# A four-layer cross-attention kernel: output projections joined two by two in PSUM, grouped layers one step later, the grouped maximum spread in SBUF

## The chip, the cores and the metric

The kernel runs on one core of one Trainium2 chip. The metric is the device time of one execution in microseconds; a run is one timed execution, and the time of the kernel before is the median of three.

## The reference, cut to what matters

Four layers of cross-attention follow each other on four sequences (b = 0 to 3) of 512 positions with 256 channels. The keys and values of all layers come from one context of 1024 positions with 512 channels for each sequence. Layers 0, 2 and 3 have 16 heads of 64 and add a penalty to four chosen keys; they are called masked below. Layer 1 has 16 query heads of 16, which share 4 key and value heads, and a root-mean-square norm ahead of the query projection; it is called grouped.

```python
# masked layer (0, 2, 3)
q = x @ Wq;  k = ctx @ Wk;  v = ctx @ Wv          # split in 16 heads of 64
logits = q k^T / 8 + col_bias                       # -20 * (1 - mask) on chosen keys
x = softmax(logits) @ v @ Wo + bo + x
# grouped layer (1)
xn = x * rsqrt(mean(x * x) + eps) * norm_w
q = xn @ wq;  k = ctx @ wk;  v = ctx @ wv           # 16 query heads, 4 shared key heads
x = x + softmax(q k^T / 4) @ v @ wo
```

All is computed in float32.

## The kernel before, in words

**Groups and steps.** A layer of a sequence is cut into eight groups (`units`): a masked group is a pair of heads, a grouped group is half of the query heads of one place r in all shared heads (h = 0 or 1). `order` puts them into 96 steps by two strings written by hand: MASKED_TURNS names the sequence whose next masked group is scored in a step, GROUPED_TURNS the sequence of its grouped group, if there is one. 96 steps have a masked group, 32 of them a grouped one too. Layers of one sequence follow each other, since a layer's query projection needs the full result of the layer before.

**What a step does.** In the loop over n, `g` is the masked group of the step, `g1` that of the step before, `lam` the grouped group, `coming` the grouped group of the next step, `follows` the masked group of the next step, `soon` the grouped group two steps on.

- `scores(g)` (L622): eight tiles of 128 keys by two heads of 512 queries. L632 multiplies into a pair of PSUM banks, ACT copies the tile to SBUF (L642), and DVE folds it into a running maximum which stays in the banks of the first tile (L646).
- DVE reduces that maximum over keys (L683, L691, L716) and `max_everywhere` spreads it over two banks (L723); eight subtractions (L728) and eight exponentials (L734) follow, and POOL adds up the exponentials (L773).
- TensorE meanwhile multiplies g1's exponentials by the values (`attend`, L662). In a step with `lam`, its scores (L611) and exponentials (L619) go pair by pair between those of g1.
- `reciprocal_sums` and `scale_out` (L787 to L815) normalise g1's product into a tile `ot`; `normalise_grouped` (L775) does so for a grouped pair that was finished in the step before (`turned`).
- `project_out` (L817) multiplies `ot` by the output weights (four matmul instructions L829) into two banks, and DVE adds them to the layer's accumulator (L851). Both happen in the step after the group was normalised. A grouped output is projected after every second grouped group.
- `project_q` (L533, matmul L543) makes the queries of the next masked group and of coming grouped ones; `k_part` (L467, grouped L485) and the value functions (L509) make keys and values.
- `maxima_pair` (L597) computes the scores of the coming grouped group once for its maximum alone; `lower_queries` (L694) reduces it, spreads it with a transposition into one PSUM bank (L706) and lowers the queries by it (L709). The bank is then given back.

**Order of the work.** The schedule is manual: each engine takes its instructions in the order in which the program issues them. `scores`, the attention of g1 and the exponentials of lam are issued first. Then a list `fill` of TensorE work is issued item by item; each has a planned length in microseconds, and DVE and ACT work is issued when the planned clock passes its due time (`events`: subtraction t at 0.7 + 1.2 t, exponential t at 3.3 + 1.22 t; `pairs`: grouped maxima from 11.0 or 12.0 on). The add behind a projection is issued when its item is done.

**PSUM.** `Place` hands out one or two of the eight banks. It takes the free bank (or pair) that was given back longest ago; `late` makes a returned bank count as returned later. So which bank a tile gets, and on whose last read it waits, follows from the order of the returns.

**Loads.** `load_masked` issues on SP, at the start of a step, the key weights of the group three steps on, the query weights two on, g's output weights (L442, four buffers) and the value weights two on.

Of the kernel before, what the change touches and what calls it, by code (L numbers as in the profile page):

```python
# [42 lines left out]
def units(b):  # L43
# [13 lines left out]
    "000000001111111122222222000000001111111100000000"  # L57
    "222222223333333311111111222233333333222233333333"
)
GROUPED_TURNS = (  # L60
    "...........00000000..11111111..22222222........."
    "...................33333333....................."
)
# [13 lines left out]
def kernel(ctx: ExitStack, tc: tile.TileContext, a: dict, out: bass.AP):  # L77
# [616 lines left out]
    def lower_queries(g):  # L694


        half = max_halves(g, g.mx)
        every = t_([P, S // 32, 1], "every1", f"every1_{g.name}")
        for c in range(4):
            cols = slice(c % 2 * S // 32, (c % 2 + 1) * S // 32)  # L700
            nc.vector.tensor_tensor(
                every[32 * c : 32 * (c + 1), :, 0], half[0:32, cols], half[32:64, cols], ALU.max
            )
        w = Place(1)
        m = w.ap
        nc.vector.transpose(  # L706
            m.rearrange("p (b r) -> p b r", r=32), every.to_broadcast([P, S // 32, 32])
        )
        nc.vector.scalar_tensor_tensor(g.qt, m, row16[:, 1:2], g.qt, ALU.mult, ALU.add)  # L709
        w.back(late=2)  # L710

# [63 lines left out]
    def normalise_grouped(g, m):  # L775
# [7 lines left out]
        )  # L783
        g.ot = t_([P, S], "ot", f"ot_{g.name}", bufs=3)
        nc.vector.tensor_tensor(g.ot, o, m, ALU.mult)

# [29 lines left out]

    def project_out(g):  # L817
        x, acc = xs[g.l, g.b], xs.get((g.l + 1, g.b))
# [9 lines left out]
        for k in range(KC):  # L828
            nc.tensor.matmul(  # L829
                m[:, k * S : (k + 1) * S], lhsT=g.wo[:, k * P : (k + 1) * P], rhs=g.ot,  # L830
                start=True, stop=True,
            )
        y = m.rearrange("p (k q) -> p k q", q=S)
# [19 lines left out]

        left[g.b] -= 1
        return add
# [36 lines left out]
    def masked_at(n):  # L892
        return masked[n] if n < len(masked) else None

    def head(g):
# [52 lines left out]
    count = 0  # L948
    ready = []
    turned = []  # L950
    left = {b: 32 - 4 for b in range(B)}

    for n in range(len(steps) + 2):
# [8 lines left out]
        def load_masked():  # L962
            if g and masked_at(g.n + 3):
                load_k(masked_at(g.n + 3))
            if g and masked_at(g.n + 2):
                load_q(masked_at(g.n + 2))
            if g:
                load_o(g)
            if g and masked_at(g.n + 2):
                load_v(masked_at(g.n + 2))  # L970
# [14 lines left out]

        outs, ready = ready, []
        events = []
# [46 lines left out]
        if turned or lam and g1:  # L1034
# [4 lines left out]
            for each in turned:  # L1039
                normalise_grouped(each, w.ap)  # L1040
            w.back(late=12)
        turned.clear()
        if lam:
            for i in range(NT // 2):
# [7 lines left out]
                if not g:  # L1052
                    if i == 1 and outs:
                        project_out(outs.pop(0))()
                    if i == 2 and queries:
                        project_q(queries.pop(0))()
# [13 lines left out]
        elif g1:  # L1070
            attend_last(g1)
            adds = [project_out(each) for each in outs]
            outs = []
# [11 lines left out]
        if coming and (g or not lam):  # L1085
# [6 lines left out]
        fill, of_grouped = (  # L1092
            [(1.8, lambda each=each: project_out(each)) for each in outs if lam or each.masked == m]
            for m in (True, False)
# [27 lines left out]
        fill += of_grouped  # L1122
        if follows and follows.l and follows.u == 0:
            fill.append((1.7, lambda: project_q(follows)))
        if soon and soon.first:
# [4 lines left out]
        if g and masked_at(g.n + 1):  # L1130
            fill += values(masked[g.n + 1])
        if g1 and g and ending:

# [56 lines left out]
```

## Time and profile before

| what | us |
|---|---|
| median of three runs | 3749.14 (3747.16 to 3749.33) |
| the profiled execution | 3746.54 |
| its span, first to last instruction | 3744.7 |
| around the span | 1.8 |
| TensorE busy | 3694.7 (99%) |
| VectorE busy | 3033.9 (81%) |
| ScalarE busy | 2105.5 (56%) |
| GpSimd busy | 1624.2 (43%) |

| steps | count | length of one, us |
|---|---|---|
| with a masked group alone (most of them) | 60 | 31.94 |
| last before a grouped layer begins | 4 | 47.4 to 48.8 |
| with a grouped group, u even | 16 | 47.9 to 52.5 |
| with a grouped group, u odd | 16 | 41.2 to 47.6 |

In the profile, PE is TensorE's multiplication, PEld its weight loads, DVE VectorE, ACT ScalarE, POOL GpSimd, SP the queue that issues most DMAs. An entry like "L829 PE MATMUL ps<-ot,wo" names the line, the engine, the operation, what is written and what is read; "[0.73 <-DVE qt L709]" says that the engine was idle for 0.73 us until that instruction released it. One float32 matmul of the program appears as two instructions. A step is measured from the first L632 of its masked group to that of the next. Some busy time is waiting: matmuls are pipelined and their ends are modelled.

### The profile page before, as it was taken

How to read it: one execution, taken by the hardware profiler on the slowest of the kernel's cores; microseconds unless marked ns; L12 is line 12 of the kernel's file. 1: busy time of each engine (PE TensorE's matmuls, PEld its weight loads, DVE VectorE, ACT ScalarE, POOL GpSimd, SP SyncE). 2: the span in 40 equal slices, each digit the busy share in tenths (PEclk: the TensorE clock that was granted, in tenths of full speed). 3: DMA queues.
4: the chain of work that ended last, by engine and by line, in shares of the span. 5: the costliest groups of instructions: out<-in, count | busy, mean ns of one | idle time of the engine just before them, and what ended most of it. 6: DMA issues, size and time to landing. Idle time of an engine off the chain costs nothing.

```text
span 3744.7 us, 48356 instructions
## 1 busy us (share of the span) xinstructions
PE 3694.7 (99%) x18606; PEld 1842.0 (49%) x18606; DVE 3033.9 (81%) x3959; ACT 2105.5 (56%) x2433; POOL 1624.2 (43%) x749
## 2 busy tenths in 40 slices
PE   8999999999999999999999999999999999999998
PEld 4555544445444454444555555554544445555554
DVE  6887788877888778887888778888788877888888
ACT  4555565555555555555555565555555555555554
POOL 3555333343333433334455555555333344555554
PEclk9999999999999999999999999999999999999999
DMA  2111110001000010000000110000100000000100
GB/s 68 43 32 27 37 31 22 18 21 25 22 22 18 21 25 22 22 18 24 25 22 26 48 37 26 26 26 20 25 22 22 18 27 23 26 26 26 32 25 8
DMA packets 187867, 98.58 MB, mean 26 GB/s; under 512 B 43240, under 2 KB 183528, under 8 KB 187636
## 3 DMA queue, kind: packets, MB, share of 16 engines
q1 hardware_dynamic: 182510, 82.90, 8.1%
q0 software_dynamic: 2560, 8.39, 0.8%
q10 hardware_dynamic: 2566, 4.20, 0.5%
q8 instruction: 147, 2.41, 0.3%
q14 instruction: 84, 0.69, 0.1%
HBM read 89.16 MB, written 2.10 MB: 24 GB/s over the span
## 4 chain that ended last, share of the span: by engine, by line
PE 90%; DVE 6%; ACT 2%; issue 1%; DMA 0%; POOL 0%; DVEq 0%; ACTq 0%; POOLq 0%
PE ps L662 20%; PE ps L509 19%; PE ps L467 17%; PE ps L632 16%; PE ps L611 8%; PE ps L829 5%; PE ps L543 3%; DVE ps L646 2%; DVE st L728 1%; ACT st L642 1%; ACT st L619 1%; PE ps L485 1%; PE ps L638 1%; DVE quarter L683 1%; DVE st L603 0%
## 5 line engine op out<-in xcount | busy, mean ns | idle before, releaser
L773 POOL TENSOR_TENSOR st<-st 128x1024 f32<-128x1024 f32 x668 | 1579.6, 2365 | 2073.6 <-ACT st L734 2029.5
L646 DVE TENSOR_TENSOR ps<-ps,st 128x1024 f32<-128x1024 f32 x672 | 828.4, 1233 | 437.4 <-ACT st L642 376.9
L734 ACT ACTIVATE st<-st 128x1024 f32<-128x1024 f32 x768 | 783.0, 1054 | 706.3 <-DVE st L728 695.0
L728 DVE TENSOR_TENSOR st<-st,ps 128x1024 f32<-128x1024 f32 x768 | 886.0, 1215 | 3.2
L662 PE MATMUL ps<-st,v 128*64 128x512 f32 x4064 | 810.9, 598 | 0.0
L509 PEld LDWEIGHTS ps<-wv,ctx 128*128 128x128 f32 x6400 | 732.0, 192 | 103.6 <-issue 91.2
L642 ACT COPY st<-ps 128x1024 f32<-128x1024 f32 x768 | 715.6, 1044 | 85.1 <-PE ps L638 68.3
L509 PE MATMUL ps<-wv,ctx 128*128 128x128 f32 x6400 | 752.8, 277 | 1.2 <-ACT st L642 0.6
L632 PE MATMUL ps<-qt,kt 64*128 64x512 f32 x3072 | 714.3, 598 | 11.1 <-DVE qt L709 6.4
L467 PE MATMUL ps<-ctx,wk 128*128 128x512 f32 x1536 | 685.6, 597 | 2.2 <-ACT ctx L379 2.2
L662 PEld LDWEIGHTS ps<-st,v 128*64 128x64 f32 x4064 | 231.2, 130 | 551.5 <-issue 477.9
L467 PEld LDWEIGHTS ps<-ctx,wk 128*128 128x128 f32 x1536 | 287.9, 190 | 387.7 <-issue 375.4
L632 PEld LDWEIGHTS ps<-qt,kt 64*128 64x128 f32 x3072 | 290.4, 186 | 340.9 <-ACT st L642 155.1
L521 ACT COPY v<-ps 128x512 f32<-128x512 f32 x200 | 117.2, 586 | 561.6 <-PE ps L509 561.5
L603 DVE TENSOR_TENSOR st<-st,ps 128x1024 f32<-128x1024 f32 x224 | 273.6, 1221 | 132.3 <-ACT st L601 69.9
L619 ACT ACTIVATE st<-ps 128x1024 f32<-128x1024 f32 x256 | 248.1, 1021 | 158.5 <-PE ps L611 119.4
L611 PE MATMUL ps<-qt,kt 32*128 32x512 f32 x2048 | 304.6, 639 | 3.3 <-DVE ot L814 3.3
L829 PE MATMUL ps<-ot,wo 128*128 128x512 f32 x448 | 218.8, 615 | 6.2 <-ACT st L619 5.5
L543 PE MATMUL ps<-x,wq 128*128 128x512 f32 x384 | 187.6, 612 | 6.4 <-ACT st L734 5.3
L611 PEld LDWEIGHTS ps<-qt,kt 32*128 32x128 f32 x2048 | 92.0, 183 | 159.1 <-ACT st L619 51.9
L829 PEld LDWEIGHTS ps<-ot,wo 128*128 128x128 f32 x448 | 77.0, 189 | 146.6 <-issue 110.4
L723 DVE STREAM_TRANSPOSE ps<-every 128x1024 f32<-128x1024 f32 x96 | 120.8, 1258 | 32.2 <-ACT st L619 24.8
(142 smaller groups left out, 1567.2 us busy)
## 6 DMA issues: line engine op xcount, KB each, us to landing
wk<-in_L_xattn_Wk_dram SPq DMA_DIRECT2D x96, 256.0 KB, 2.9
wv<-in_L_xattn_Wv_dram SPq DMA_DIRECT2D x96, 256.0 KB, 2.9
wq<-in_L_xattn_Wq_dram SPq DMA_DIRECT2D x96, 128.0 KB, 2.9
wo<-in_L_xattn_Wo_dram SPq DMA_DIRECT2D x96, 128.0 KB, 3.0
qt<-qt ACTq DMA_DIRECT2D x32, 128.0 KB, 2.2
xraw<-in_x_dram SPq DMA_DIRECT2D x3, 512.0 KB
out_dram<-out SPq DMA_DIRECT2D x3, 512.0 KB
wq<-in_L_xattn_wq_dram SPq DMA_DIRECT2D x32, 32.0 KB, 3.2
```

Source lines behind the costliest of these rows:

```text
L467: nc.tensor.matmul(m, lhsT=g.wk[:, k, :], rhs=ctx_t[g.b][:, k, n * 512 : (n + 1) * 512], start=(k == 0), stop=(k == KT - 1),)
L509: nc.tensor.matmul(m[:, t * P : (t + 1) * P], lhsT=ctx_t[g.b][:, k, (4 * n + t) * P : (4 * n + t + 1) * P], rhs=g.wv[:, k, :], start=(k == ...
L543: nc.tensor.matmul(m, lhsT=g.wq[:, k, :], rhs=x[:, k, :], start=(k == 0), stop=(k == KC - 1))
L611: nc.tensor.matmul(ws[odd].ap[:, j * S : (j + 1) * S], lhsT=g.kt[rows, i * P : (i + 1) * P], rhs=g.qt[rows, :], start=True, stop=True,)
L632: nc.tensor.matmul(m[:, j * S : (j + 1) * S], lhsT=g.kt[g.rows[j], keys], rhs=g.qt[g.rows[j], :], start=True, stop=t > 0,)
L642: nc.scalar.copy(g.st[t], m)
L646: nc.vector.tensor_tensor(top, top, g.st[t], ALU.max)
L662: nc.tensor.matmul(g.po[at, :], lhsT=g.v[:, t, rows], rhs=g.st[t][:, j * S : (j + 1) * S], start=(t == first), stop=(t == last),)
L728: nc.vector.tensor_tensor(g.st[t], g.st[t], g.mb, ALU.subtract)
L734: nc.scalar.activation(st, st, AF.Exp)
L773: nc.gpsimd.tensor_tensor(g.acc, g.st[0] if t == 1 else g.acc, g.st[t], ALU.add)
L829: nc.tensor.matmul(m[:, k * S : (k + 1) * S], lhsT=g.wo[:, k * P : (k + 1) * P], rhs=g.ot, start=True, stop=True,)
```

## The change

Five things are edited together.

1. Both strings are rewritten: every grouped sequence begins one step later, and the last layer of batch 2 is cut after five groups instead of four, so that the last sequence of layer 2 begins a step later as well.
2. `project_out` takes one or two groups. A masked group with even u is held until the next one of the same layer and sequence is ready; both are then multiplied into the same two banks, accumulating in PSUM, with one add. The last two masked groups of the program are not joined. With the first edit these joined projections come in the steps that have no grouped projection. The output weights are loaded one step later to fit.
3. `lower_queries` spreads the grouped maximum over the first half of the tile it was collected in (`g.mx`, in SBUF) instead of a PSUM bank, and takes no place.
4. `normalise_grouped` writes its product over its input instead of a new `ot` tile, and the bank of `reciprocal_sums` is returned with `late=12` only where a grouped pair was normalised in it.
5. The query projection of the first group of a later layer moves to just ahead of the last item of `fill`, a quarter of the value projection.

```diff
 MASKED_TURNS = (
     "000000001111111122222222000000001111111100000000"
-    "222222223333333311111111222233333333222233333333"
+    "222222223333333311111111222223333333322233333333"
 )
 GROUPED_TURNS = (
-    "...........00000000..11111111..22222222........."
-    "...................33333333....................."
+    "............00000000..11111111..22222222........"
+    "....................33333333...................."
 )
...
-        w = Place(1)
-        m = w.ap
+        m = g.mx[:, 0:S]
         nc.vector.transpose(
             m.rearrange("p (b r) -> p b r", r=32), every.to_broadcast([P, S // 32, 32])
         )
         nc.vector.scalar_tensor_tensor(g.qt, m, row16[:, 1:2], g.qt, ALU.mult, ALU.add)
-        w.back(late=2)
...
-        g.ot = t_([P, S], "ot", f"ot_{g.name}", bufs=3)
-        nc.vector.tensor_tensor(g.ot, o, m, ALU.mult)
+        g.ot = o
+        nc.vector.tensor_tensor(o, o, m, ALU.mult)
...
-    def project_out(g):
+    def project_out(*of):
+        g = of[0]
...
         for k in range(KC):
-            nc.tensor.matmul(
-                m[:, k * S : (k + 1) * S], lhsT=g.wo[:, k * P : (k + 1) * P], rhs=g.ot,
-                start=True, stop=True,
-            )
+            for each in of:
+                nc.tensor.matmul(
+                    m[:, k * S : (k + 1) * S], lhsT=each.wo[:, k * P : (k + 1) * P], rhs=each.ot,
+                    start=each is g, stop=each is of[-1],
+                )
...
-        left[g.b] -= 1
+        left[g.b] -= len(of)
...
+    def with_next(g):
+        other = masked_at(g.n + 1)
+        return other and other is not masked[-1] and (other.l, other.b) == (g.l, g.b)
...
-            if g:
-                load_o(g)
+            if g1:
+                load_o(g1)
...
-        outs, ready = ready, []
+        outs = []
+        for each in ready:
+            if each.masked and each.u % 2 == 0 and with_next(each):
+                held.append(each)
+            else:
+                outs.append(held + [each] if each.masked else [each])
+                if each.masked:
+                    held = []
+        ready = []
...
-            w.back(late=12)
+            w.back(late=12 if turned else 0)
...
-            [(1.8, lambda each=each: project_out(each)) for each in outs if lam or each.masked == m]
+            [
+                (1.8 * len(each), lambda each=each: project_out(*each))
+                for each in outs if lam or each[0].masked == m
+            ]
...
-        if follows and follows.l and follows.u == 0:
-            fill.append((1.7, lambda: project_q(follows)))
...
             fill += values(masked[g.n + 1])
+        if follows and follows.l and follows.u == 0:
+            fill[-1:-1] = [(1.7, lambda: project_q(follows))]
```

## The prediction

> **What bounds the kernel now.** Busy times and the chain of waits come first. In both the reader is to see that TensorE carries the end.
>
> ```profile
> PE 3694.7 (99%) x18606; PEld 1842.0 (49%) x18606; DVE 3033.9 (81%) x3959; ACT 2105.5 (56%) x2433; POOL 1624.2 (43%) x749
> ...
> PE 90%; DVE 6%; ACT 2%; issue 1%; DMA 0%; POOL 0%; DVEq 0%; ACTq 0%; POOLq 0%
> ```
>
> A busy PE may still be held up, so I cut the trace into steps (step n begins with the first score matmul, L632, of masked group n) and read four: 24 and 25 with a grouped group, 46 without one, 75 at the hand-over to the last layer-2 sequence.
>
> ```profile
> 1039.90:1086.10 46.20, 46.03 (x253) 20.47 (x252) 35.99 (x44) 27.54 (x31) 16.80 (x8) 1.00 0.03 7
> 1086.10:1137.60 51.50, 50.60 (x259) 22.18 (x259) 45.65 (x63) 28.53 (x33) 16.82 (x8) 1.00 0.12 31
> 1972.60:2004.50 31.90, 31.90 (x155) 17.04 (x154) 26.37 (x34) 18.03 (x21) 16.50 (x8) 1.00 0.09 26
> 3055.00:3096.60 41.60, 36.29 (x162) 18.92 (x160) 29.68 (x39) 18.10 (x21) 19.01 (x9) 0.92 0.07 20
> ```
>
> Columns: length, PE, weight loads, DVE, ACT, POOL, granted clock and DMA. Step 46 is PE from end to end, with DVE 5.5 us in hand; step 25 leaves DVE 5.9 us in 51.5. So an edit can gain only where PE waits. The timelines of TensorE (steps 46 and 25) and of the hand-over show where:
>
> ```profile
> 1972.58 1.13 PE L632 MATMUL ps<-qt,kt 64*128 64x512 f32 x4
> ...
> 1979.86 7.09 PE L662 MATMUL ps<-st,v 128*64 128x512 f32 x32
> ```
> ```profile
> 1086.08 1.13 PE L632 MATMUL ps<-qt,kt 64*128 64x512 f32 x4
> ...
> 1090.72 4.56 PE L632 MATMUL ps<-qt,kt 64*128 64x512 f32 x18 [0.73 <-DVE qt L709]
> 1095.21 1.94 PE L662 MATMUL ps<-st,v 128*64 128x512 f32 x8
> ...
> 1107.23 1.98 PE L543 MATMUL ps<-x,wq 128*128 128x512 f32 x4
> ```
> ```profile
> 3078.10 1.88 PE L829 MATMUL ps<-ot,wo 128*128 128x512 f32 x4
> ...
> 3083.97 1.22 DVE L851 TENSOR_TENSOR x<-ps,x 128x1024 f32<-128x1024 f32 x1
> ...
> 3085.29 3.75 PE L543 MATMUL ps<-x,wq 128*128 128x512 f32 x4 [5.31 <-ACT st L734]
> ```
>
> Scores take 7.28 us in step 46 and 9.13 in step 25, where a bank holds the spread maximum until L709. At the hand-over, the query projection waits for a DVE add that stands behind eight subtractions.
>
> **The change, part by part.**
>
> *Pairs.* 46 pairs form (96 masked groups less four singles: two where batch 2's last layer is cut, two at the end). Each drops one DVE add of 1.22 us (L851) and one two-bank place: 56 us of DVE. The matmuls stay 448. In steps like 46 the four L829 run 1986.88 to 1988.70 (1.82) and the four L543 behind them 1.72: 2 x 3.54 = 7.08 per two steps. Paired: 1.82 in the step without an output (L543 comes first and pays the 0.10 that the first matmul after a change of tile shape costs), then 3.54 + 1.72: 7.08. Worth 0. DVE's 5.5 us hide anything smaller there.
>
> *Step later.* Groups with odd u now meet grouped ones with odd u, so the masked pair falls into steps without a grouped output. PE work moves from the heavy step (25: eight L829) to the light one (24: four), 1.72 us each way: 0 by itself. DVE loses 1.22 per two steps. In odd-u steps its add now waits for eight matmuls instead of four, some 0.9 us, with five subtractions and their exponentials queued behind it; those steps have no grouped normalisation (2.4 us of DVE: 0.68 + 0.26 + 0.73 + 0.69), which covers it. Uncovered, it would come back at the first L611: 16 x 0.9 = 14 us.
>
> *Maximum in SBUF.* L706 into SBUF should take 0.711 (L803, same form) for 0.727, L709 with two SBUF inputs 0.751 (L275, same form) for 0.751: 32 x 0.016, nothing. What counts is the bank. Over the 32 grouped steps, scores exceed 7.29 us by: 0.57 four times (12, 22, 32, 68), 0.61 three times (18, 28, 38), 0.98 five times (23, 27, 33, 37, 73), 1.84 five times (15, 17, 25, 35, 71), 1.93 (13) and 2.19 (69): 22.2 us before rounding. The large ones wait for L709 itself; the small ones come in steps whose fourth score tile reuses the pair of the second, since held or late-returned banks leave only two pairs to turn over (it then waits for ACT's copy). In the changed kernel's built order no grouped step does that and no score waits for L709: -22.2. Two steps without a grouped group still do (41, 77), as 40 and 76 did.
>
> Where the stall goes: next late is the first pair of grouped maxima, whose second place is freed by the last subtraction. In step 25 the subtractions end at 1121.75 and L611 starts at 1121.94: 0.2 us spare. Changed: L603 ends some 1.1 us before the step, L709 about 2.8 after its start (now 4.6), the seven L646 at 12.7 (now 13.8), the transposed maximum 10.1 later at 22.8, then eight subtractions at 1.14 and one add: 33.1; the pair is due at 34.0 (7.29 + 12.03 attention and exponentials, 2.15 queries, 3.63 output and grouped query, 3.57 grouped attention, 5.35 keys). Spare 0.9; nothing comes back. The even-u step has the least room.
>
> *The port.* The Trainium skill (SBUF — State Buffer, "Who interferes with whom") speaks against this edit: a DVE instruction with two SBUF inputs contends with a GpSimd instruction that reads SBUF, and the later one blocks until the first ends. This case agrees: four of the eight L590 started during a POOL add.
>
> ```profile
> L590 DVE SCALAR_TENSOR_TENSOR xn<-x,colL_xattn_norm_w,inv x8: 736/991/2792, 366.7 to 2623.4; 128x512 f32<-128x512 f32 x8
> ```
> ```profile
> 1066.93 17.02 POOL L773 TENSOR_TENSOR st<-st 128x1024 f32<-128x1024 f32 x7 [32.23 <-ACT st L734]
> ...
> 1118.32 14.57 POOL L773 TENSOR_TENSOR st<-st 128x1024 f32<-128x1024 f32 x6 [0.93 <-ACT st L734]
> ```
>
> By the rule with an add under way, L709 costs up to 2.79 - 0.74 = 2.05 more, 66 us for 32; by where the rows lie, 0: adds end 2.1 us (step 24) and 4.7 us (25) before the next step, and L709 will start some 2.0 after its start. I take 0, bounds 0 and +66. Behind a held L709 queue the seven L646; exponentials and then PE's next places would wait.
>
> *Bank return (late=12 only if one was turned).* In all 32 grouped steps the first output matmul waits for the last exponential ("PE ps L829 <- ACT st L619: 5.5, 32" among the waits): four L543 then last 2.15 instead of 1.82, and L829 pays 0.10: 0.44. Built order: in 13 odd-u steps it now waits for the exponential before that (in step 25 ACT runs the two from 1107.40 to 1109.34, so the earlier ends at 1108.4; the matmul would be due at 1109.05), and four first steps have no output: 17 x 0.44 = -7.5. In steps 23, 39 and 71 the query moved away and eight output matmuls follow the exponentials directly, due 1107.2: +0.8 net each, +2.4. Together -5.1; bounds -14 and +2.
>
> *Query moved before the last value quarter.* Step 75 took 41.41; 31.94 plus a second output (1.72) is 33.66: 7.75 lost, 0.4 of it because the clock fell (0.92 mean). Changed (step 76): from the end of attention, first subtraction at 4.4, seven in 8.0, add to 13.5; PE reaches the query at 6.97 + 1.72 + 5.43 = 14.1. -7.75. Step 39 likewise: 34.51 - 33.66 = -0.85. Same tile shape on both sides of the query, so no switch is paid; its copy (0.59) has 1.8 us to the next scores.
>
> *End.* Step 94 loses an output: PE 1.72, DVE 1.2. The last step's scores, maxima and exponentials follow that earlier; its pair's eight matmuls (3.6) fit before the first exponential except about 0.2: -1.0; bounds -1.7 and 0.
>
> *At nothing:* output weights loaded a step later on SP (0.46 to issue, 3.0 to land; at least one step of 31.9 us remains, and the value weights behind them are not used before the next step); four buffers still turn over, as each one's last reader ran a step before. In-place product in o: the next write of o (L672) follows grouped attention, which stands behind the output projection on PE. If that cover failed, each would cost its 3.0 or 0.6 us.
>
> **Sum.** -22.2 - 5.1 - 7.75 - 0.85 - 1.0 = -36.9. Span 3744.7 becomes 3707.8, the profiled execution 3746.54 becomes 3709.6; the median of the runs, 2.6 above that execution, 3749.14 becomes 3712.
>
> **Rivals.** (a) The stall moves. If DVE in even-u steps starts no earlier, the subtractions free the pair's bank later than PE wants it: the larger score waits (1.93 + 9.2 + 2.19 + 4.9 = 18.2) come back at L611. For: 0.2 us spare now. Against: L709 leaves 1.8 us sooner, an add drops out. 3730. (b) Slower, by the port: all 32 L709 held 2.0 us with nothing hiding it: +64 - 37 = +27, 3776; it beats the gain once more than 1.16 us of each hold reaches PE. It needs the adds to run four to five microseconds later against the step than now; nothing in the change delays them that much. (c) The change doesn't do what it says: score waits are ACT's pace, not banks, and only the hand-overs and the end gain: 9.6 us, 3739.5. Against: scores without any wait run 7.28 with the same ACT copies.
>
> **Numbers.** Forecast 0.62 (3703 to 3721); (a) 0.24 (3721 to 3736); (c) 0.05; less than that, within 0.2% 0.03; (b) 0.04, of which I leave 0.01 to no change; more gained than forecast 0.02. 0.2% (7.5 us) is about what a measurement can tell from no change. Faster 0.93, same 0.04, slower 0.03. Range 3703 to 3733: the forecast's, and (a) up to 3 us beyond its time.
>
> **What would show it.** Right: scores near 7.29 in every grouped step; even- and odd-u steps near 47.9 and 47.6; no wait above 1 us at the projection ahead of the last layer-2 sequence; masked steps still 31.94. Wrong: L709 above 0.8 us; L611 behind L727; output matmuls still behind the last exponential in odd-u steps.

## The result, and the profile after

| | before | after |
|---|---|---|
| median of five runs each, us | 3748.74 | 3708.30 (3707.82 to 3709.47) |
| ratio, with its 95% interval | 1 | 0.9893 (0.9879 to 0.9906) |
| span of the profiled execution | 3744.7 | 3706.5 |

Predicted were 3712, from a sum of -36.9. The spans differ by 38.2, the medians by 40.4. Ratios here and below leave out slow executions, of which there was one: 15330 us, with the maximum alone. First, from the page of the changed kernel, the engines' busy times and the shares of the chain of work that ended last.

```profile
PE 3675.1 (99%) x18606; PEld 1835.8 (50%) x18606; DVE 2979.7 (80%) x3913; ACT 2109.5 (57%) x2433; POOL 1624.8 (44%) x749
...
PE 95%; DVE 3%; ACT 1%; issue 1%; DMA 0%; POOL 0%; ACTq 0%; DVEq 0%; POOLq 0%
```

TensorE issues as many matmuls as before, DVE 46 additions fewer. In the chain of work that ended last, DVE's share fell from 6% to 3% and TensorE's rose from 90% to 95%. These shares follow one chain and don't measure the gain: 3% of the span are 111 us. Next the stretches of five steps (columns as in the prediction; the last number is GB/s): 24 (u even), 25 (u odd), 46 and 47 (masked alone, without and with a pair) and 76, the last ahead of layer 2 of the last sequence. Every grouped group sits one step later than before, so steps with even u have even numbers now: 24 is to be compared with a step like old 25.

```profile
1011.97:1059.92 47.95, 47.78 (x256) 21.09 (x255) 39.76 (x49) 28.40 (x33) 16.80 (x8) 1.00 0.06 16
1059.92:1107.42 47.50, 47.50 (x255) 21.18 (x254) 39.16 (x51) 27.66 (x31) 16.84 (x8) 1.00 0.12 30
1950.06:1980.29 30.23, 30.23 (x152) 16.30 (x151) 25.25 (x33) 18.10 (x21) 13.18 (x7) 1.00 0.09 27
1980.29:2013.94 33.65, 33.65 (x159) 17.82 (x158) 26.37 (x34) 18.18 (x21) 19.89 (x9) 1.00 0.07 20
3057.62:3089.56 31.94, 31.94 (x155) 17.06 (x154) 27.25 (x37) 17.86 (x21) 9.21 (x4) 1.00 0.07 22
```

The two grouped steps are alike now, and TensorE waits for 0.17 us in one and nowhere in the other. Steps 46 and 47 together last 63.88, as two masked steps did before. From the timeline of step 24, which began at 1011.97, DVE and TensorE:

```profile
1011.47 0.71 DVE L706 STREAM_TRANSPOSE st<-every 128x512 f32<-128x512 f32 x1
...
1012.22 0.75 DVE L709 SCALAR_TENSOR_TENSOR qt<-st,row,qt 128x512 f32<-128x512 f32 x1
...
1013.15 6.17 PE L632 MATMUL ps<-qt,kt 64*128 64x512 f32 x28
...
1037.05 8.00 DVE L727 TENSOR_TENSOR st<-st,ps 128x1024 f32<-128x1024 f32 x7
...
1045.99 1.14 PE L611 MATMUL ps<-qt,kt 32*128 32x512 f32 x8
```

The 28 score matmuls run through without a break. The last subtraction (L727 now) ends at 1045.05 and the first pair of grouped maxima (L611) starts at 1045.99: 0.94 us to spare (0.58 in step 70, the least of the even-u steps), and its eight instructions take 1.14. L709 comes unusually early here, 0.25 us into the step; in most even-u steps it starts 1.96 to 2.02 in. L646 starts at 3.39 all the same, because it waits for ACT's copies (L642), so L709 has some 0.6 us of room of its own. That pair is the place to watch in all that follows. The hand-over, step 76:

```profile
3078.89 1.88 PE L831 MATMUL ps<-o,wo 128*128 128x512 f32 x4
3080.61 5.52 PE L509 MATMUL ps<-wv,ctx 128*128 128x128 f32 x48
3084.22 1.22 DVE L853 TENSOR_TENSOR x<-ps,x 128x1024 f32<-128x1024 f32 x1
3085.35 1.21 DVE L727 TENSOR_TENSOR st<-st,ps 128x1024 f32<-128x1024 f32 x1
3085.97 1.88 PE L543 MATMUL ps<-x,wq 128*128 128x512 f32 x4
```

Three quarters of the values now lie between the output and the query, and the add ends 0.5 us ahead of the query that needs it.

### The profile page after: what moved, and what is told of

It reads as the page before. It is cut to its first block, busy times and chain, and to the rows that moved or that the text cites. A ratio compares the mean times of both kernels' runs of the same rounds, so it can differ in the third digit from the quotient of the medians.

```text
span 3706.5 us, 48343 instructions
## 1 busy us (share of the span) xinstructions
PE 3675.1 (99%) x18606; PEld 1835.8 (50%) x18606; DVE 2979.7 (80%) x3913; ACT 2109.5 (57%) x2433; POOL 1624.8 (44%) x749
## 4 chain that ended last, share of the span: by engine, by line
PE 95%; DVE 3%; ACT 1%; issue 1%; DMA 0%; POOL 0%; ACTq 0%; DVEq 0%; POOLq 0%
PE ps L662 21%; PE ps L509 20%; PE ps L467 18%; PE ps L632 17%; PE ps L611 8%; PE ps L831 5%; PE ps L543 5%; DVE ps L646 1%; DVE st L727 1%; PE ps L485 1%; PE ps L638 1%; ACT st L642 0%; ACT st L619 0%; PE ps L373 0%; PE ps L582 0%
## 5 line engine op out<-in xcount | busy, mean ns | idle before, releaser
L646 DVE TENSOR_TENSOR ps<-ps,st 128x1024 f32<-128x1024 f32 x672 | 828.5, 1233 | 466.9 <-ACT st L642 404.4
L727 DVE TENSOR_TENSOR st<-st,ps 128x1024 f32<-128x1024 f32 x768 | 882.3, 1215 | 3.2
L662 PE MATMUL ps<-st,v 128*64 128x512 f32 (+1 forms) x4064 | 810.9, 598 | 0.0
L642 ACT COPY st<-ps 128x1024 f32<-128x1024 f32 x768 | 713.2, 1051 | 69.2 <-PE ps L638 68.4
L632 PE MATMUL ps<-qt,kt 64*128 64x512 f32 x3072 | 702.2, 596 | 1.3 <-ACT st L642 0.7
L662 PEld LDWEIGHTS ps<-st,v 128*64 128x64 f32 (+1 forms) x4064 | 231.2, 130 | 551.5 <-issue 468.1
L611 PE MATMUL ps<-qt,kt 32*128 32x512 f32 x2048 | 304.9, 639 | 2.5 <-DVE ot L813 1.2
L549 ACT ACTIVATE qt<-ps 128x512 f32<-128x512 f32 x96 | 56.9, 593 | 251.3 <-PE ps L543 251.3
L543 PE MATMUL ps<-x,wq 128*128 128x512 f32 x384 | 188.3, 613 | 1.1 <-ACT x L351 1.1
L831 PE MATMUL ps<-ot,wo 128*128 128x512 f32 x384 | 176.8, 602 | 4.3 <-ACT st L619 3.5
L611 PEld LDWEIGHTS ps<-qt,kt 32*128 32x128 f32 x2048 | 90.2, 182 | 159.8 <-ACT st L619 51.9
L472 ACT COPY kt<-ps 128x512 f32<-128x512 f32 x192 | 110.5, 575 | 49.2 <-PE ps L467 43.2
```

The costliest lines, as they stand in the source:

```text
L543: nc.tensor.matmul(m, lhsT=g.wq[:, k, :], rhs=x[:, k, :], start=(k == 0), stop=(k == KC - 1))
L611: nc.tensor.matmul(ws[odd].ap[:, j * S : (j + 1) * S], lhsT=g.kt[rows, i * P : (i + 1) * P], rhs=g.qt[rows, :], start=True, stop=True,)
L632: nc.tensor.matmul(m[:, j * S : (j + 1) * S], lhsT=g.kt[g.rows[j], keys], rhs=g.qt[g.rows[j], :], start=True, stop=t > 0,)
L642: nc.scalar.copy(g.st[t], m)
L646: nc.vector.tensor_tensor(top, top, g.st[t], ALU.max)
L662: nc.tensor.matmul(g.po[at, :], lhsT=g.v[:, t, rows], rhs=g.st[t][:, j * S : (j + 1) * S], start=(t == first), stop=(t == last),)
```

## The experiments

Ratios are to the kernel before. For reading the twelve, each profiled execution was cut into stretches: what lies ahead of the first score (opening), the 32 grouped steps, the four steps that lead into a grouped layer (11, 21, 31, 67; 10, 20, 30, 66 without the shift), and the rest.

| kernel | median | opening | 32 grouped | 4 lead-in | rest | span |
|---|---|---|---|---|---|---|
| before | 3748.7 | 33.2 | 1527.9 | 191.1 | 1992.6 | 3744.7 |
| changed | 3708.3 | 33.8 | 1497.7 | 198.2 | 1976.9 | 3706.5 |
| maximum alone | 3741.4 | 35.0 | 1520.2 | 192.6 | 1992.6 | 3740.4 |
| turns alone | 3746.5 | 34.0 | 1526.2 | 191.1 | 1993.3 | 3744.5 |
| pairs alone | 3810.4 | 34.0 | 1590.5 | 186.4 | 1998.1 | 3809.0 |
| changed, maximum in PSUM | 3730.3 | 33.9 | 1516.6 | 197.8 | 1977.7 | 3726.0 |
| changed, no pairs | 3723.7 | 33.6 | 1512.0 | 190.4 | 1985.2 | 3721.1 |
| changed, no shift | 3741.0 | 34.3 | 1530.5 | 184.5 | 1990.1 | 3739.4 |
| changed, product apart | 3710.0 | 34.6 | 1497.7 | 199.8 | 1976.9 | 3708.9 |
| changed, query early | 3720.3 | 35.4 | 1497.7 | 201.6 | 1984.9 | 3719.5 |
| changed, always late | 3716.7 | 35.2 | 1503.4 | 198.2 | 1977.5 | 3714.2 |
| changed, POOL beside L709 | 3710.5 | 33.6 | 1498.7 | 199.8 | 1976.9 | 3709.0 |
| changed, outputs later | 3701.9 | 34.8 | 1490.2 | 198.1 | 1976.9 | 3700.0 |
| and pairs of maxima later | 3698.4 | 34.8 | 1490.6 | 193.3 | 1978.1 | 3696.8 |

The opening differs by up to 2.2 us between executions in which no instruction of it differs, and single lead-in steps come in two lengths 1.6 us apart (more on this at the end). So a difference under some 3 us between two spans is not put down to an edit. The grouped steps repeat better: 1497.7 with the changed kernel and with the query early, whose code there is the same, and 0.4 us apart in the last two rows.

**The maximum in SBUF, alone.** Is the bank worth 22.2 us by itself?

```diff
 # in the kernel before
-        w = Place(1)
-        m = w.ap
+        m = g.mx[:, 0:S]
...
-        w.back(late=2)
```

> The kernel before with the grouped maximum spread in SBUF and nothing else changed. The bank theory (the scores of 32 grouped steps lose 22.2 us because the spread maximum keeps a PSUM bank until L709): 22.2 us less than before, about 3726.5, with L706 near 0.71 us and L709 near 0.75, and scores near 7.29 us in the grouped steps. The rival that the stall moves to the first pair of grouped maxima (which ends only 0.2 us to spare in this kernel, since its DVE add and steps are unchanged): more than half of it comes back at L611, about 3738 or more. The rival that the score waits are the pace of the copies: about 3748. The rival of the shared port: above 3750, with L709 over 1 us.

Measured: ratio 0.9979 (0.997 to 0.9987), 3741.4; the grouped steps are 7.7 us shorter. Yet the scores take 7.29 us now (7.50 in step 38 alone): the whole 22.2 us have gone from them, and 14.5 came back. From the timelines of TensorE and DVE in step 15 (u even, 617.00 to 668.05):

```profile
618.18 6.17 PE L632 MATMUL ps<-qt,kt 64*128 64x512 f32 x28
...
647.39 3.70 PE L467 MATMUL ps<-ctx,wk 128*128 128x512 f32 x8
646.49 5.74 DVE L726 TENSOR_TENSOR st<-st,ps 128x1024 f32<-128x1024 f32 x5
651.02 2.40 PE L611 MATMUL ps<-qt,kt 32*128 32x512 f32 x8
653.34 1.98 PE L467 MATMUL ps<-ctx,wk 128*128 128x512 f32 x4
655.26 1.27 PE L611 MATMUL ps<-qt,kt 32*128 32x512 f32 x8
```

The reader is to compare 2.40 with the 1.14 of an undisturbed L611: TensorE arrives 1.84 us sooner, and the pair's second place is still held by the last subtraction, which ends at 652.23 (L726 here). No wait is printed, because most of it counts as the busy time of the matmuls; it shows in the sum of the group, 304.6 us before, and here:

```profile
L611 PE MATMUL ps<-qt,kt 32*128 32x512 f32 x2048 | 316.9, 639 | 5.0 <-DVE ot L812 3.3
```

That is 12.3 us of busy time and 1.7 of idle time more: 14.0 of the 14.5 us. The forecast's rival (a), the stall that moves, is what happens when this edit stands alone.

**The change without it.**

```diff
 # in the changed kernel
-        m = g.mx[:, 0:S]
+        w = Place(1)
+        m = w.ap
...
+        w.back(late=2)
```

> The changed kernel with the spread maximum back in a PSUM bank that is returned late. The bank theory: slower than the changed kernel by 10 to 16 us, 3718 to 3724, less than the 22.2 us of the kernel before because L703 and the spread now come nearer to the step's beginning, and because in 15 of the 32 grouped steps the fourth score tile has to take the second one's pair again (0.6 to 1.0 us each). The rival that the shifted order alone had removed the score waits: 3708, no difference. The rival of the port (two SBUF inputs cost something here): faster than 3708.

Measured: ratio 0.9951 (0.9939 to 0.9964), 3730.3, 22.0 above the changed kernel: the bank theory holds, but its size was too low (10 to 16). The grouped steps are 18.9 us longer, every bit of it in their scores. Waits for the transposed maximum, not only reused pairs, are back (from the groups by line):

```profile
L632 PE MATMUL ps<-qt,kt 64*128 64x512 f32 x3072 | 711.6, 598 | 11.6 <-ACT st L642 5.9 <-DVE qt L710 4.8 <-DVE ot L815 0.6
```

In eight steps with u = 1 or 7 the scores lose 0.98 to 1.94 us, 11.5 together, where L710 itself (L709 of the changed kernel) is late: the steps ahead of them, u = 0 and 6, have one projection less, end with only 1.98 us of value work behind their last pair of maxima, and so L709 falls deeper into the next step. The expectation had counted only the 15 steps with a reused pair.

**No pairs.**

```diff
 # in the changed kernel
-            if each.masked and each.u % 2 == 0 and with_next(each):
+            if False:
```

> The changed kernel with each masked output projected by itself, in every step, as before the change; all else as changed. This puts back 46 DVE additions of 1.22 us and 46 two-bank places, with the same 448 output matmuls. The theory that the pairs are worth nothing by themselves in masked steps, and that in even-u grouped steps they leave DVE its 0.9 us of slack ahead of the first pair of grouped maxima: 0 to 6 us slower than the changed kernel, about 3708 to 3714. The rival that DVE's 56 us carry the gain: 20 to 40 us slower, 3728 to 3748.

Measured: ratio 0.9934 (0.9922 to 0.9947), 3723.7, 15.4 above the changed kernel; too large for the expectation, too small for the rival. Lead-in steps and the rest only exchange outputs (-7.8 and +8.3, so the pairs are worth nothing there); the grouped steps are 14.3 us longer. Step 14 (548.21 to 599.26), DVE and TensorE:

```profile
551.96 0.75 DVE L709 SCALAR_TENSOR_TENSOR qt<-st,row,qt 128x512 f32<-128x512 f32 x1
...
577.70 5.74 DVE L727 TENSOR_TENSOR st<-st,ps 128x1024 f32<-128x1024 f32 x5
582.23 2.40 PE L611 MATMUL ps<-qt,kt 32*128 32x512 f32 x8
```

L709 starts 3.75 us into the step; in the changed kernel's step 14 it starts at 2.02. The odd-u step ahead is one output lighter and ends 1.98 us behind its last pair of maxima instead of 3.77. So the seven L646 start 1.03 later, one more add lies between the subtractions and moves the rest by 1.13, and the last of these ends at 35.23 instead of 33.07; L611 is due at 34.02. The expectation had counted the add and forgotten the shorter step.

**No shift.**

```diff
 # in the changed kernel: the two strings as before the change
-    "222222223333333311111111222223333333322233333333"
+    "222222223333333311111111222233333333222233333333"
...
-    "............00000000..11111111..22222222........"
-    "....................33333333...................."
+    "...........00000000..11111111..22222222........."
+    "...................33333333....................."
```

> The changed kernel without the shift: the grouped layers begin where they did before, so the masked pairs fall into the even-u grouped steps beside a grouped output; maximum in SBUF and product in place as changed. The theory that the shift is what gives DVE its room: in the built order the odd-u steps end with their last pair of grouped maxima, so L709 comes some 3.8 us later in the even-u step than in the changed kernel, and one more add of 1.15 us lies among the subtractions; with 0.9 us of slack that leaves TensorE waiting 3 to 4 us at the first pair of grouped maxima of some 12 even-u steps: 35 to 55 us slower than the changed kernel, 3743 to 3763. The rival that the shift no longer matters once the maximum holds no bank: 3708, within 5 us.

Measured: ratio 0.9981 (0.9973 to 0.9989), 3741.0, 32.7 above the changed kernel, a little under the range; the grouped steps are 32.8 longer. L709 starts 5.73 us into step 15, as expected 3.7 later. But the wait is split: in step 15 1.7 us come already inside the attention and 1.5 at the first pair of maxima, as the timeline shows. All twelve even-u steps from u = 2 on have the first of these waits, 1.6 us of it idle:

```profile
633.59 1.14 PE L611 MATMUL ps<-qt,kt 32*128 32x512 f32 x8 [1.62 <-DVE quarter L683]
...
652.30 1.13 PE L611 MATMUL ps<-qt,kt 32*128 32x512 f32 x4
653.86 1.13 PE L611 MATMUL ps<-qt,kt 32*128 32x512 f32 x4 [0.43 <-DVE st L727]
```

A grouped score waits for the reduction of the running maximum (L683), which stands behind the late L646.

**Turns alone.**

```diff
 # in the kernel before: the two strings as in the changed kernel
-    "222222223333333311111111222233333333222233333333"
+    "222222223333333311111111222223333333322233333333"
...
-    "...........00000000..11111111..22222222........."
-    "...................33333333....................."
+    "............00000000..11111111..22222222........"
+    "....................33333333...................."
```

> The kernel before with the grouped layers begun one step later and nothing else changed. The theory that the shift by itself brings nothing (the same outputs meet the same grouped groups, the maximum still holds a bank, the query at the hand-over still waits): within 5 us of the kernel before, 3744 to 3754. The rival that the shift carries the part of the gain that the maximum alone left out: about 3730.

Measured: ratio 0.9996 (0.9988 to 1.0004), 3746.5: the shift by itself is worth nothing that can be told apart, though without it 33 of the 40 us are gone.

**Pairs alone.** The code for pairs, and the output weights loaded a step later, in the kernel before.

```diff
-        outs, ready = ready, []
+        outs = []
+        for each in ready:
+            if each.masked and each.u % 2 == 0 and with_next(each):
+                held.append(each)
...
-            if g:
-                load_o(g)
+            if g1:
+                load_o(g1)
```

> The kernel before with masked outputs in pairs, but the grouped layers not shifted and the maximum still in PSUM, so that the pairs fall into the even-u grouped steps, beside a grouped output (12 output matmuls there, none in the odd-u steps). The theory that this is the wrong place: in the built order the odd-u steps then end with their last pair of grouped maxima, so L709 comes some 2 us later in the following even-u step than now and holds its bank for that much longer: 15 to 35 us slower than before, about 3764 to 3784, with scores of 11 us or more in the even-u steps. The rival that fewer additions on DVE (46 x 1.22 us) are what matters, wherever the pairs fall: 10 to 20 us faster than before.

Measured: ratio 1.0165 (1.0151 to 1.0179), 3810.4, 61.8 slower, well beyond the range, though the scores of the even-u steps from u = 2 on take 9.4 to 10.3 us and not 11. Something else was missed: the product of `normalise_grouped` (L785 here), by the trace of its line.

```profile
L785 DVE TENSOR_TENSOR ot<-o,ps x16: 686/689/689, 545.4 to 3137.7; 128x512 f32<-128x512 f32 x16
...
  PE ps L832: 39.1, 12
```

In twelve even-u steps DVE stands still for up to 4.2 us, 39.1 in all, until the pair's matmuls have read the held masked output: three `ot` buffers don't suffice for a held output, its partner and a grouped one. Scaling, spread maximum and eight subtractions queue behind it. So this run prices two things, the wrong place and the missing buffer; the run without the shift above has the product in place (and the maximum in SBUF), so it has the wrong place without the missing buffer.

**Product apart.** Is the in-place product needed in the changed order too?

```diff
 # in the changed kernel
-        g.ot = o
-        nc.vector.tensor_tensor(o, o, m, ALU.mult)
+        g.ot = t_([P, S], "ot", f"ot_{g.name}", bufs=3)
+        nc.vector.tensor_tensor(g.ot, o, m, ALU.mult)
```

> The changed kernel with the normalised grouped output in a buffer of its own again (one of three shared with the masked outputs) instead of in place. The theory of the prediction, that the in-place product is worth nothing in the shifted order, where no write to these buffers waits for TensorE in the built order: 3708, within 2 us. The rival that the masked output held for its pair takes one of three buffers, so that the grouped product waits for the pair's matmuls as it did by 4 us in the kernel before with pairs alone: 40 us slower or more.

Measured: ratio 0.9897 (0.9882 to 0.9912), 3710.0 (3708.0 to 3712.6); the grouped steps are the same to 0.1 us. With the shift the pair is projected in steps without a grouped product, and the edit is worth nothing, as forecast.

**Query early.**

```diff
 # in the changed kernel
+        if follows and follows.l and follows.u == 0:
+            fill.append((1.7, lambda: project_q(follows)))
...
-            fill[-1:-1] = [(1.7, lambda: project_q(follows))]
```

> The changed kernel with the query projection of the first grouped group of a layer-2 sequence back where it was, ahead of the values instead of ahead of their last quarter. The theory that this projection waits there for eight subtractions and an add, and nothing hides it: 7 to 9 us slower than the changed kernel, about 3715 to 3717, nearly all of it in the last masked step of layer 1 (some 40 to 41 us long instead of 31.9). The rival that the shifted order alone took away that wait: 3708, no difference.

Measured: ratio 0.9921 (0.9908 to 0.9934), 3720.3, 12.0 above the changed kernel and more than expected. Step 76 takes 39.84 instead of 31.94, the wait that was expected:

```profile
3081.27 8.00 DVE L727 TENSOR_TENSOR st<-st,ps 128x1024 f32<-128x1024 f32 x7
...
3089.19 1.22 DVE L853 TENSOR_TENSOR x<-ps,x 128x1024 f32<-128x1024 f32 x1
...
3090.51 3.75 PE L543 MATMUL ps<-x,wq 128*128 128x512 f32 x4 [4.76 <-issue]
```
```profile
3090.00:3096.00 6.00, 5.49 (x14) 3.46 (x15) 5.58 (x13) 1.71 (x3) 5.84 (x3) 0.50 0.09 25
```

The view puts it down to "issue", but L543 starts 0.1 us after the add on which its input depends, and that add stands behind seven subtractions. Of the 7.9 us 4.9 are this wait. The rest is paid behind it: the clock granted to TensorE falls to 0.50 near the end of the wait and stays there to 3096 (second view), so the query takes 3.54 us for 1.72 and the values 8.38 for 7.24. Another 3.3 us lie in two lead-in steps (11 and 67), where the same 1.6 us turn up in kernels without this edit.

**Always late.**

```diff
 # in the changed kernel
-            w.back(late=12 if turned else 0)
+            w.back(late=12)
```

> The changed kernel with the bank of the normalisation always returned twelve places late, as before the change. The theory that the early return lets 13 odd-u steps project their outputs without waiting for the last exponential, worth 0.44 us each: 4 to 7 us slower than the changed kernel, about 3714, with a wait of 0.33 us ahead of L831 in the odd-u steps too. The rival that the outputs would wait no matter which bank comes back: 3708, no difference.

Measured: ratio 0.9915 (0.9901 to 0.9928), 3716.7, 8.4 above the changed kernel. Odd-u steps go from 47.51 to 47.94, 13 times 0.43, which is the 5.7 us of the theory but for rounding (grouped steps 1497.7 to 1503.4). Another 0.6 lies in the rest, 1.4 in the opening, which the edit doesn't touch.

**POOL beside L709.** The rival of the shared port, made to happen. This kernel does additions on POOL that no output needs.

```diff
 # in the changed kernel, ahead of L706
+        tiny = t_([P, S // 32], "tiny", f"tiny_{g.name}")
+        nc.gpsimd.tensor_tensor(tiny, every[:, :, 0], every[:, :, 0], ALU.add)
+        for _ in range(2):
+            nc.gpsimd.tensor_tensor(g.mx[:, S:], g.mx[:, S:], g.mx[:, S:], ALU.add)
```

> The changed kernel with three more instructions on POOL at each spread of a grouped maximum: a tiny add that reads what the spread reads, so that POOL gets there at the same time as DVE, and two additions of 128x512 in SBUF on a part of the maxima that nothing reads any more. So the multiply-add L709, with its two SBUF inputs, meets a POOL instruction that reads SBUF in all 32 grouped steps. The theory of the shared port: L709 lasts 1.5 to 2.8 us instead of 0.75, and since the first pair of grouped maxima has only 0.9 us to spare in even-u steps, part of it reaches TensorE: 5 to 25 us slower than the changed kernel, about 3713 to 3733. The rival that slack covers it: longer L709, but 3708. The rival that the two engines do not hold each other up with this operation: L709 stays at 0.75 and the time at 3708.

Measured: ratio 0.9899 (0.9883 to 0.9914), 3710.5, 2.2 above the changed kernel, of which the grouped steps hold 1.0. By the timeline (L713 is L709 here):

```profile
446.89 0.71 DVE L710 STREAM_TRANSPOSE st<-every 128x512 f32<-128x512 f32 x1
...
447.11 2.48 POOL L708 TENSOR_TENSOR st<-st 128x512 f32<-128x512 f32 x2
447.64 1.06 DVE L713 SCALAR_TENSOR_TENSOR qt<-st,row,qt 128x512 f32<-128x512 f32 x1
...
551.53 9.26 DVE L646 TENSOR_TENSOR ps<-ps,st 128x1024 f32<-128x1024 f32 x7 [0.24 <-ACT st L642]
```

The hold is real: all 32 take 1.055 to 1.058 us instead of 0.75. The first POOL add ends 0.51 us after L713 started, and L713 ends 0.55 us after that. So 9.8 us of DVE time cost TensorE 1.0: the covered rival, and a smaller hold than expected, because the add met was 1.04 us long and half over.

Where the cover lies can be read from L646. In most grouped steps DVE idles ahead of it for some 0.6 us until ACT's copies are there; with the hold 0.24 are left (last line, step 14), L646 starts as before, and these steps are no longer. Only in the eight steps with u = 1 or 7 does L646 follow L709 without a pause: there it starts about 0.4 us later, and all of the 1.0 us is theirs (0.43 in step 13, 0.05 to 0.08 in the others). A hold of the 2 us that a 128x1024 add would give was not tried. An estimate from these numbers is some 18 us, not the 64 of the forecast's rival (b): all but 0.3 us of each hold in those eight steps, and what goes beyond 0.6 us of cover ahead of L646 and 0.9 ahead of L611 in nine even-u steps.

**Outputs later.** Waits of the first output matmul remain in the changed kernel: 0.33 us in twelve even-u steps, 1.33 in steps 23, 39 and 71.

```diff
 # in the changed kernel, steps with lam
+        outs, of_outs = [], fill
+        if lam:
+            fill = []
...
         fill += of_queries
         if lam:
+            if popped:
+                fill += of_outs
...
             fill.append((3.6, attend_grouped))
+            if not popped:
+                fill += of_outs
```

`popped` is set where a masked query was already projected inside the attention, so that a grouped one is left to go ahead of the outputs.

> The changed kernel with the outputs of grouped steps projected later: behind the remaining query projection, and in the three steps where no query is left behind grouped attention. All else as changed. The theory that the output matmuls still wait for the last exponential of the grouped attention (0.33 us in nine or more even-u steps, 1.33 us in steps 23, 39 and 71, plus 0.1 for a change of tile shape) and that work put ahead of them hides this: 5 to 9 us faster than the changed kernel, about 3700 to 3703. The rival that the later DVE add delays the subtractions and the wait comes back at the first pair of grouped maxima: 3708 or slower.

Measured: ratio 0.9876 (0.9861 to 0.9891), 3701.9 (3701.2 to 3703.2), 6.4 below the changed kernel; the grouped steps are 7.5 us shorter: 8 even-u steps 0.43 each, steps 23, 39 and 71 4.0 together; the four with u = 6 are unchanged. Nothing comes back at L611. Of the outputs from grouped tiles, 2.1 us of idle time ahead of them became 0.7:

```profile
L831 PE MATMUL ps<-o,wo 128*128 128x512 f32 x64 | 30.7, 602 | 0.7 <-ACT st L619 0.7
```

**And pairs of maxima later.**

```diff
 # in the kernel with outputs later
-            pairs += [((12.0 if lam else 11.0 if g else 0.0) + 2.5 * i, i) for i in range(NT // 2)]
+            pairs += [((12.0 if lam else 12.5 if g else 0.0) + 2.5 * i, i) for i in range(NT // 2)]
```

> The kernel with outputs later (the run before this one) and one number changed: in the four steps ahead of a grouped layer (11, 21, 31, 67) the pairs of grouped maxima are placed one piece of key or value work later (12.5 for 11.0). The theory that these steps wait 0.6 to 1.4 us each at L611 for the last subtractions, 3.6 us in all, and that a piece of work ahead of it hides that: 3 to 4 us faster than the kernel with outputs later, about 3698.5. The rival that the first scores or the next step's first maxima come late in turn: 3702, no difference.

Measured: ratio 0.9866 (0.9849 to 0.9882), 3698.4 (3697.4 to 3698.6). The lead-in steps are 4.8 us shorter, and L611, 304.9 us of busy and 2.5 of idle time in the changed kernel, is free of waits:

```profile
L611 PE MATMUL ps<-qt,kt 32*128 32x512 f32 x2048 | 302.6, 640 | 0.0
```

This kernel is the fastest of all here.

## Why the prediction was right, point by point

**Scores, -22.2.** Measured: their excess over 7.29 us went from 22.2 to -0.2. Right, but only in company. By leaving out one edit at a time, the maximum in SBUF is worth 22.0 us, the shift 32.7, the pairs 15.4; alone, the first two are worth 8.0 and 2.1 (not to be told from nothing), and pairs alone cost 61.8. These sum to more than the 40.4 because each needs the others: the bank frees the scores, and DVE reaches its last subtraction sooner by 2.2 us through the pairs and by 4.1 through the shift (it ends 33.07 us into an even-u step, 35.23 without the pairs, 37.21 without the shift). Without that room the freed time returns at L611.

**Where the stall goes.** The step that decided. The sum gave the last subtraction at 33.1 and L611 due at 34.0 in even-u steps; step 14 has 33.07 and 34.02. L709 ends 2.77 us into it (2.8), L646 at 12.64 (12.7), the spread maximum at 22.77 (22.8). One thing the prediction had wrong about the kernel before: it took the 0.2 us to spare in step 25 for the general case. In five steps (23, 27, 33, 37, 73) TensorE already waited there for the last subtraction, 0.35 us each. Step 23, from the timelines of DVE and TensorE:

```profile
1019.56 4.61 DVE L728 TENSOR_TENSOR st<-st,ps 128x1024 f32<-128x1024 f32 x4
...
1023.86 1.49 PE L611 MATMUL ps<-qt,kt 32*128 32x512 f32 x8
```

The pair takes 1.49 us instead of 1.14. The changed kernel has no such wait in a grouped step.

**Pairs 0, shift 0.** Right as sums of TensorE's time: 30.23 + 33.66 in masked steps for 2 x 31.94, and the shift alone is within 0.2%. But the working had these two as parts worth nothing and DVE's room as a detail of another part. A reader who had dropped either for its 0 would have lost 15 or 33 us. The add in odd-u steps waited 0.78 us in four of them (17, 25, 37, 73), 0.43 and 0.30 in two (15, 71), and at most 0.05 in the others; as expected, none of it came back.

**Bank return, -5.1.** The 13 odd-u steps measure 5.7 us when it is undone, and steps 23, 39 and 71 did get the new wait: 1.33 us where 0.33 had been, 1.24 longer than their neighbours, so +0.8 net each.

**Query, -7.75 and -0.85.** Steps 76 and 40 are 31.94; undoing it costs 7.9 in step 76. The total was right, its split wrong: the prediction gave the clock 0.4 of it, but the 3.55 us of the query behind the wait in old step 75 were half clock too (0.50 granted from 3083 to 3089), so some 2.3 were the clock's and 5.4 the wait's:

```profile
3083.00:3089.00 6.00, 3.71 (x5) 1.68 (x6) 5.72 (x13) 2.14 (x3) 5.77 (x4) 0.50 0.00 0
```

**End, -1.0.** Step 94 is 1.72 us shorter, step 95 0.54 longer: -1.18.

**The port, 0.** L709 took 0.750 to 0.753 in every grouped step, L706 0.711 to 0.714. POOL was kept out by place, not by nature: put beside it, it holds L709 by 0.31. The Trainium skill (SBUF — State Buffer, "Who interferes with whom") says of such a pair that the later one waits until the first ends, and the measurement fits: L709 ended only 0.55 us after the POOL add had ended.

**Nothing for loads and the in-place product.** Right in this order: no output matmul waits for a load in the trace, and the product apart costs nothing. In the unshifted order a product in its own buffer waits 39.1 us.

**What the sum missed.** Of the 3.9 us between 3712.2 and 3708.3, 2.6 come from the end of the sum: it added to the span the distance by which the median of the kernel before lay above its profiled execution, and the changed kernel's profiled execution is its own median. The other 1.3 are on spans: the grouped steps lost 30.2 where the terms add up to 27.3, the other steps lost 8.6 for 9.6, and the opening was 0.6 longer. Two things account for 2.6 of the 2.9 in the grouped steps. The five waits of 0.35 above are gone, 1.75 us, a gain that the sum had at nothing. And a piece of transpositions (L373, 0.84 us) runs in step 11 in both kernels; step 11 was a grouped step and is a lead-in one now, so this piece has only changed columns, and it is most of what the other steps fell short.

Rivals: (a) is real without shift or pairs, and absent with both; (b) needs a meeting that the order doesn't make; (c) falls, since the scores lost 22.2 us when the bank was freed and took 18.9 again when it was used.

## What to carry to other kernels

Follow the engine that frees the next resource through the whole step, to its last instruction ahead of the next wait, and set that against when the freed engine will arrive: two end times 0.9 us apart decided 14 us here. Look at every step of the kind, not at one: the step that was read had 0.2 us to spare where five others already waited. A part worth nothing by itself may be what makes another part worth anything, so price edits both alone and left out. A wait can sit in an instruction group's busy time: compare the group's sum or a single duration with an undisturbed one before believing an empty wait column.

## What the runs showed of the hardware

- A multiply-add of DVE with two SBUF inputs that starts while POOL adds in SBUF is held: it ends 0.55 us after the POOL add ends, for the 512-wide add (1.06 us in all) and for L590 behind a 1024-wide one (up to 2.79 in the kernel before, 2.84 in the changed one). The POOL add that began during the held L713 took 1.37 us instead of 1.04. The transposition L710 beside a POOL add kept its 0.71.
- The same code loses 1.6 us of clock in some executions and not in others. Step 11 took 50.23 us in the changed kernel and 51.83 with the product apart, which differs nowhere in that step. The first stretch below is from the kernel with the product apart, the second from nearly the same place in the changed kernel:

```profile
432.80:436.20 3.40, 3.40 (x9) 1.01 (x8) 2.95 (x5) 1.80 (x2) 3.24 (x3) 0.59 0.00 0
```
```profile
433.00:436.00 3.00, 3.00 (x19) 1.43 (x18) 2.84 (x4) 1.33 (x2) 2.92 (x2) 1.00 0.00 0
```

TensorE is busy throughout both, but at a mean granted clock of 0.59 in the first (9 matmuls in 3.4 us) and of 1.00 in the second (19 in 3.0). The low clock lasts about 3.3 us and begins some 3 us behind the first L611 with its two waits, 0.43 and 0.08 us. The changed kernel has the same two waits there and kept its clock, so they don't decide it alone. The Trainium skill (TensorE: Matmul & The Clock Gate, "What's actually happening") has a free-running window of about 3.4 us, which fits the length and that the same code meets it only at times; but it asks for a whole window of idling, and the trace has 0.5 us of it near this place (the page's section on a second failure mode names short idling between groups, without a length). What sets the low clock off was not tried and is not shown. The openings, which differ by 2.2 us, are not explained either.
